# A spline convolution written out as a fixed software pipeline, with the silu products of two strips packed on 64x32 tiles of TensorE

## The chip, the cores and the metric

The kernel is one launch on one core of a Trainium2 chip. The metric is the device time of the launch in microseconds (us); lower is better.

## The reference, cut to what matters

The network has four layers on an array of 8 images, 16 channels and 256 by 256 pixels, each of the form `x = x + layer(groupnorm(x))`: a capsule convolution (layer 0), a spline convolution (layer 1), a patch attention (layer 2) and a 3x3 convolution written with Fourier transforms (layer 3). Only layer 1 is touched:

```
patches = _extract_patches(x, KSIZE, STRIDE, PAD)          # 3x3 neighbourhoods
bspl = _b_splines(patches, grid)                           # 8 cubic splines per value
base_w = base_weight.sum(axis=2)
spl_w = (spline_weight * spline_scaler[..., None]).sum(axis=2)
out = jnp.einsum('bjhwn,ijn->bihw', jax.nn.silu(patches), base_w)
out = out + jnp.einsum('bjhwns,ijns->bihw', bspl, spl_w)
out = out + bias_weight[None, :, None, None]
```

So each output pixel is a 3x3 convolution over 16 channels of silu(x), plus a 3x3 convolution over 16 channels times 8 splines, plus a bias and the residual.

## The kernel before

Layer 1 walks over 8 images of 16 strips each, 128 strips in all; a strip is 16 rows of an image. All data are fp32.

**Per strip, the features.** A tile `xr` holds the input rows of the strip, once for each of four pairs of splines on its 128 partitions. It is worked on in groups of 4 rows pairs, 128x1024 elements each: two groups a strip, and a third, small one (128x256) in the last strip of an image. ScalarE (ACT in the profile) takes two absolute values, `distance` (L1021) and `other` (L1024), into `d`. VectorE (DVE) clips `d` in two ways into `a` and `e` (L1032). ACT squares each into PSUM (`sq`, L1038), DVE multiplies them to cubes (L1041). GpSimd (POOL) subtracts, which gives one half of the splines, `v` (L1050), and DVE makes the other half from it, `m` (`right`, L1053). Both halves lie in a ring of three tiles, `bases`. At the first and last strip of an image a padding row is set as well (`outside`, L1058). ACT also makes two tiles of silu values a strip (L1091).

**Per strip, the products.** One PSUM tile `ps` (one bank; there are two) collects the strip's outputs: 128 partitions are four groups of 32, n = 0 to 3, of two output rows and 16 channels. Each TensorE (PE) product takes a stationary matrix of 128 rows by 32 columns, so four products, n = 0 to 3, lie beside each other on the array. A round is four such products of 512 columns. There are 12 rounds on `bases` (2 values of q, 2 kinds, 3 of dx), the later six of which need the first rows of the next strip too, and three rounds on silu (dx), with a stationary matrix `wm` of 128 rows that holds zeros for the input rows which an output row does not touch. All have the line L1115. Then DVE adds bias and residual (L1152), takes statistics (L1164), and SyncE's queue (SPq) stores the strip.

**Order.** Nothing is written out by hand: each step is handed to a planner, `_Order`, with an estimated duration, its reads and writes and a count of buffers (`places`, `banks`), and the planner sets the order of the instructions on each engine. Its operations with `mode="shared"` are those of DVE and POOL that it keeps apart. The strips are admitted at a period that is given:

```
places = dict(xr=3, d=3, a=3, e=3, res=4, rs=4, y=2)
banks = dict(sq=3, ps=2)
order = _Order({**places, **banks}, 13.3)
```

```
for n in range(len(todo) + 1):
    ...
    if n < len(todo):
        features(*todo[n], op)
    if n:
        conv_strip(*todo[n - 1], op)
    if n < len(todo):
        silus(*todo[n], op)
    ahead(n, op)
```

Ahead of the first strip the weights are summed on PE (L947 and, for silu, L972) and spread by DVE. Within the last strips some steps of layer 2 are run: its norm's statistics (`stats2_steps`), its weights and its first patches. Layer 2 starts once the last strip of layer 1 is stored.

Of the kernel before, what the change touches and what calls it, by code (L numbers as in the profile page):

```python
# [17 lines left out]
P = 128  # L18
# [13 lines left out]
def _consts():  # L32
# [19 lines left out]
    for i in range(C):  # L52
# [32 lines left out]
        "keep": np.stack([p >= 16, p < 112, p >= 64, p < 64], 1),  # L85
# [44 lines left out]
def _layout(w0, bw, sw, sc, bias, wq, bq, wk, bk, wv, bv, w3):  # L130
# [17 lines left out]
    main = np.zeros((8, C, 9, 3, 4, 2, C), np.float32)  # L148
    for ro in range(8):
        for dh in range(3):  # L150

            ri = ro + dh - 1 + (1 if ro < 6 else -1)
            main[ri, :, :, :, ro // 2, ro % 2] = bt[:, :, dh]
    main = main.reshape(P, 9 * 3 * P)
# [151 lines left out]
class _Net:  # L306
# [544 lines left out]
    def layer1(self, bc, bc4, images=range(B), strips=range(16)):  # L851
# [7 lines left out]
        with ExitStack() as st:  # L859
# [3 lines left out]
            wm = one.tile([P, 3, 4, 2 * C], F32, name="wm")  # L863
# [38 lines left out]
            places = dict(xr=3, d=3, a=3, e=3, res=4, rs=4, y=2)  # L902
            banks = dict(sq=3, ps=2)
            order = _Order({**places, **banks}, 13.3)

            def buf(kind, shape):
                n = {**places, **banks}[kind]
                pool = psum if kind in banks else sbuf
                return _Buf(kind, lambda: pool.tile(shape, F32, name=f"{kind}1", tag=kind, bufs=n))

            held = {}

            def edges(i, op):
                def pads():
                    for kind in range(2):
                        for col in (0, WP - 1):
                            nc.gpsimd.tensor_copy(
                                ring[i][:, kind, :, col : col + 1],
                                pad[:, kind : kind + 1].unsqueeze(1).to_broadcast([P, 9, 1]),
                            )  # L920

                op("POOL", 1.0, pads, [], [("place", i)])

            def prepare(op):

                at1, at2 = (ring[i].rearrange("p k m w -> p (k m w)") for i in (1, 2))
                sw, sc, main = at2[:, :2592], at2[:, 2592:3888], at1[:, :3456]
                ws = one.tile([P, 2, 3, 3, C], F32, name="ws")
                wf = ws.rearrange("p k h w o -> p (k h w o)")
                ps = buf("sq", [P, 1024])  # L930
                edges(0, op)

                first = dict(sw=3.5, sc=1.8, main=4.6, b1=0.5)
                for name, t in (("sw", sw), ("sc", sc), ("main", main), ("b1", b1)):
                    op("SP", first[name], lambda name=name, t=t: nc.sync.dma_start(out=t, in_=self.d[name]), [], [(name,)], lag=3.0)

                def scaled():
                    for k in range(2):
                        nc.vector.tensor_tensor(
                            sw[:, k * 1296 : k * 1296 + 1296], sw[:, k * 1296 : k * 1296 + 1296], sc, ALU.mult  # L940
                        )

                def sums():

                    for k in range(2):
                        for m in range(9):
                            nc.tensor.matmul(  # L947
                                ps()[:, k * 144 : k * 144 + 144],
                                self.k["ident"],
                                sw[:, k * 1296 + m * 144 : k * 1296 + m * 144 + 144],  # L950
                                start=m == 0,
                                stop=m == 8,
                            )

                def finish():
                    nc.vector.tensor_copy(wf, ps()[:, :288])
                    nc.vector.tensor_tensor(wf[:, 144:], wf[:, 144:], wf[:, :144], ALU.subtract)
                    nc.vector.tensor_scalar(wf, wf, 1.0 / 6.0, None, ALU.mult)
                    nc.vector.memset(tw, 0.0)

                    for k in range(2):
                        for q in range(2):
                            for h in range(2):
                                for ro in range(2):
                                    dh = 2 * q + h - ro
                                    if 0 <= dh < 3:
                                        lanes = slice(64 * h, 64 * h + 64)
                                        nc.vector.tensor_copy(tw[lanes, k, q, :, ro, :], ws[lanes, k, dh])

                def sums_main():  # L970
                    for m in range(9):
                        nc.tensor.matmul(  # L972
                            ps()[:, 512:896],
                            self.k["ident"],
                            main[:, m * 384 : m * 384 + 384],
                            start=m == 0,
                            stop=m == 8,
                        )

                op("DVE", 2.9, scaled, [("sw",), ("sc",)], [("sw",)], mode="shared")  # L980
                op("PE", 6.0, sums, [("sw",)], [(ps, 0), ("place", 2)])
                op("DVE", 3.5, finish, [(ps, 0)], [("tw",)], mode="shared")
                op("PE", 7.0, sums_main, [("main",)], [(ps, 1), ("place", 1)])


                def finish_main():
                    nc.vector.tensor_copy(wm.rearrange("p d n m -> p (d n m)"), ps()[:, 512:896])

                op("DVE", 0.5, finish_main, [(ps, 1)], [("wm",)], mode="shared")
                for i in (1, 2):  # L990
                    edges(i, op)

            def features(b, j, op):

                i = b * 16 + j
                t = ring[i % 3]
                pairs = 9 if j == 15 else 8
                xr = buf("xr", [P, 9 * W])

                def fetch():  # L1000
                    nc.sync.dma_start(
                        out=xr()[:, : pairs * W],
                        in_=self.x1p[b, :, :, 8 * j : 8 * j + pairs]
                        .rearrange("h c m w -> (h c) (m w)")
                        .unsqueeze(1)
                        .to_broadcast([2 * C, 4, pairs * W]),
                    )

                op("SP", 0.5 if i > 2 else 2.8, fetch, [], [(xr, 0)], lag=6.0 if i else 8.0)
                if not i:  # L1010
                    prepare(op)
                for p in range(0, pairs, 4):
                    n = min(4, pairs - p)
                    us = 0.2 + 0.8 * n / 4
                    d, a, e = buf("d", [P, 1024]), buf("a", [P, 1024]), buf("e", [P, 1024])
                    part = lambda t, n=n: t()[:, : n * W]
                    xn = lambda p=p, n=n: xr()[:, p * W : (p + n) * W]
                    rows = lambda ap: ap.rearrange("p (m w) -> p m w", w=W)

                    def distance(d=d, xn=xn, part=part):  # L1020
                        nc.scalar.activation(part(d), xn(), AF.Abs, bias=bd[:, b : b + 1], scale=sd[:, b : b + 1])  # L1021

                    def other(d=d, part=part):
                        nc.scalar.activation(part(d), part(d), AF.Abs, bias=minus2)  # L1024

                    op("ACT", 1.2 * us, distance, [(xr, 0)], [(d, 0)])
                    op("ACT", 1.15 * us, other, [(d, 0)], [(d, 0)])

                    for q, end, scale in ((a, 2.0, 1.0), (e, 1.0, 2.0)):

                        def less(q=q, d=d, end=end, part=part):
                            nc.vector.tensor_scalar(part(q), part(d), end, end, ALU.min, ALU.subtract)  # L1032

                        op("DVE", 0.68 * us, less, [(d, 0)], [(q, 0)], mode="shared")
                        sq = buf("sq", [P, 1024])

                        def square(q=q, sq=sq, scale=scale, part=part):
                            nc.scalar.activation(part(sq), part(q), AF.Square, scale=scale)  # L1038

                        def cube(q=q, sq=sq, part=part):  # L1040
                            nc.vector.tensor_tensor(part(q), part(q), part(sq), ALU.mult)  # L1041

                        op("ACT", 1.03 * us, square, [(q, 0)], [(sq, 0)])
                        op("DVE", 1.24 * us, cube, [(q, 0), (sq, 0)], [(q, 0)])
# [24 lines left out]
                    if end is not None:  # L1069
                        op("DVE", 0.7, outside, [], [("v", i % 3, p), ("m", i % 3, p)], mode="shared")  # L1070
# [638 lines left out]
```

## Time and profile before

| what | value |
|---|---|
| median of 3 runs | 7611.7 us (7608.63 to 7614.55) |
| the profiled execution | 7613.15 us, of which 7611.4 us are the span that the profiler recorded |
| first to last product of layer 1 (L1115) | from 4343.6 us to 6110.3 us of the span |
| busy in 4343 to 6111 us (1768 us) | PE 1680.3, DVE 1478.1, ACT 1264.9, POOL 737.3 us |
| granted TensorE clock there | 0.98 of full |
| DMA there | 154 GB/s, 0.49 of the engines' time |

How to read it: a row of the groups gives the line, engine and operation, the tiles written and read, the shape (for PE the rows and columns of the stationary matrix, then the moving data), and how often it ran; then busy time and mean time of one instruction. One fp32 product is two matmul records. A record's duration includes a tail in which the next instruction of the engine already runs, so times from start to start are shorter. "Idle before" names what ended a wait. Line numbers are those of the kernel before.

### The profile page before, as it was taken

The page shows a single profiled execution, that of the slowest core. Times are in us where ns is not written, and L with a number is a line of the kernel's source. Part 1 is how long each engine was busy: PE and PEld are TensorE (multiplying, and loading weights), DVE is VectorE, ACT ScalarE, POOL GpSimd, SP SyncE. Part 2 cuts the span into 40 slices and gives each one's busy share as a digit, 9 for nine tenths or more (in the row PEclk, how much of TensorE's full clock was granted, in tenths as well). Part 3 has the DMA queues.
Part 4 walks back from the last instruction along what each step waited for, and adds up shares of the span by engine and source line. Part 5 has one row for each costly group of instructions (what it writes and reads, how often), then busy time and mean ns, then how long its engine had stood idle before and what let it go on. Part 6 is the DMA issues. An engine that isn't in the chain of part 4 may idle for free.

```text
span 7611.4 us, 105952 instructions
## 1 busy us (share of the span) xinstructions
PE 6891.6 (91%) x43144; PEld 3281.4 (43%) x43144; DVE 5416.4 (71%) x6463; ACT 2692.1 (35%) x3834; POOL 3248.3 (43%) x1884
## 2 busy tenths in 40 slices
PE   4888888999989999899998599999999999999999
PEld 1333333333333333333333355444544566666634
DVE  5778888887888888888878788888888833333322
ACT  1222222222222222222222377777777712112200
POOL 0545555555555555555555444444444411111100
PEclk9989999999999999999999699999999999999999
DMA  6222222222222222222222354444445533333277
GB/s 243 66 66 78 78 78 77 77 77 74 77 76 77 76 77 78 78 78 78 78 78 55 103 165 154 151 153 155 150 154 159 159 116 96 86 86 97 67 215 190
DMA packets 451065, 813.01 MB, mean 107 GB/s; under 512 B 57490, under 2 KB 299282, under 8 KB 415250
## 3 DMA queue, kind: packets, MB, share of 16 engines
q1 hardware_dynamic: 380946, 738.85, 33.8%
q10 hardware_dynamic: 69632, 67.39, 3.1%
q8 instruction: 340, 5.57, 0.3%
q14 instruction: 147, 1.20, 0.0%
HBM read 595.63 MB, written 211.03 MB: 106 GB/s over the span
## 4 chain that ended last, share of the span: by engine, by line
PE 52%; POOL 21%; DVE 16%; issue 4%; ACT 3%; DMA 3%; SPq 0%; POOLq 0%; DVEq 0%; ACTq 0%
PE ps L1115 13%; POOL dd L765 11%; PE cv L545 8%; POOL s L765 8%; PE pqk L1474 6%; PE p3s L1585 4%; DVE dd L756 4%; PE cv L549 4%; PE pl L654 3%; PE po L1501 3%; PE pv L1481 3%; PE psc L1489 3%; PE fb L622 3%; POOL s L810 2%; ACT sq L1038 1%
## 5 line engine op out<-in xcount | busy, mean ns | idle before, releaser
L765 POOL TENSOR_TENSOR dd<-dd 128x1024 f32<-128x1024 f32 x512 | 1206.4, 2356 | 1594.9 <-DVE dd L756 1574.8
L1115 PE MATMUL ps<-bases,tw 128*32 128x512 f32 (+1 forms) x13824 | 1379.7, 550 | 89.0 <-DVE bases L1058 71.1
L756 DVE SCALAR_TENSOR_TENSOR dd<-rb,v 128x1024 f32<-128x1024 f32 (+1 forms) x1024 | 1076.9, 1085 | 204.6 <-PE rb L745 194.8
L554 ACT COPY v<-cv 128x1024 f32<-128x1024 f32 x512 | 518.3, 1012 | 1911.0 <-PE cv L549 1911.0
L1050 POOL TENSOR_TENSOR bases<-e,a 128x1024 f32<-128x1024 f32 (+1 forms) x264 | 745.4, 2825 | 1040.5 <-DVE e L1041 870.5
L545 PE MATMUL cv<-kt,w 128*128 128x512 f32 x2048 | 1092.4, 659 | 38.5 <-DVE dd L756 28.7
L1115 PEld LDWEIGHTS ps<-bases,tw 128*32 128x32 f32 x13824 | 734.9, 109 | 743.9 <-issue 442.1
L644 DVE TENSOR_TENSOR pr<-v,fb 128x2048 f32<-128x2048 f32 (+1 forms) x512 | 1020.5, 2017 | 24.9 <-PE pl L654 20.0
L745 PE MATMUL rb<-rs,ct_fold 32*128 32x512 f32 x3584 | 795.8, 657 | 8.3 <-ACT rs L727 2.7
L765 POOL TENSOR_TENSOR s<-s,dd 128x512 f32<-128x512 f32 x512 | 652.0, 1274 | 29.9
L545 PEld LDWEIGHTS cv<-kt,w 128*128 128x128 f32 x2048 | 366.9, 199 | 600.1 <-issue 388.2
L549 PE MATMUL cv<-kt,w 64*128 64x512 f32 x2048 | 590.2, 653 | 0.0
L654 PE MATMUL pl<-pr,ct_fold 128*32 128x512 f32 x3584 | 528.1, 613 | 59.5 <-DVE pr L644 58.7
L1468 POOL TENSOR_TENSOR t<-t,emb 128x512 f32<-128x512 f32 x128 | 161.8, 1264 | 958.4 <-DVE t L1464 943.6
L622 PEld LDWEIGHTS fb<-f,ct_fold 128*128 128x128 f32 x3072 | 377.0, 195 | 340.7 <-issue 299.2
L622 PE MATMUL fb<-f,ct_fold 128*128 128x128 f32 x3072 | 436.5, 290 | 90.1 <-DVE f L608 88.2
L1474 PE MATMUL pqk<-w_qk,t 128*128 128x512 f32 x1024 | 483.0, 594 | 4.4 <-POOL t L1468 4.4
L765 POOL TENSOR_TENSOR s<-v,dd 128x512 f32<-128x512 f32 x256 | 328.7, 1284 | 318.6 <-DVE dd L756 318.5
L1485 ACT ACTIVATE vt<-pv,w_b2v 128x128 f32<-128x128 f32 x512 | 146.0, 368 | 837.0 <-PE pv L1481 837.0
L1505 DVE TENSOR_TENSOR y<-po,res 128x512 f32<-128x512 f32 x128 | 88.5, 692 | 486.8 <-PE po L1501 486.8
L745 PEld LDWEIGHTS rb<-rs,ct_fold 32*128 32x128 f32 x3584 | 240.7, 187 | 380.1 <-DVE dd L756 211.7
L1041 DVE TENSOR_TENSOR e<-e,sq 128x1024 f32<-128x1024 f32 (+1 forms) x264 | 315.2, 1194 | 98.4 <-ACT sq L1038 98.4
(254 smaller groups left out, 9002.0 us busy)
## 6 DMA issues: line engine op xcount, KB each, us to landing
kt<-d SPq DMA_DIRECT2D x256, 516.0 KB
xr<-x1p SPq DMA_DIRECT2D x120, 1024.0 KB
rs<-x SPq DMA_DIRECT2D x256, 256.0 KB
d<-dn ACTq DMA_DIRECT2D x64, 516.0 KB
xs<-in_x_dram SPq DMA_DIRECT2D x16, 2048.0 KB
xs<-in_x_dram SPq DMA_DIRECT2D x64, 512.0 KB
res<-in_x_dram SPq DMA_DIRECT2D x64, 512.0 KB
x<-s SPq DMA_DIRECT2D x128, 256.0 KB
```

The costliest lines, as they stand in the source:

```text
L545: nc.tensor.matmul(ps()[:, n], w[:, 0, j, :], t[:, a : a + 2, 0:W], start=True, stop=False)
L549: nc.tensor.matmul(ps()[:, n], w[at, 1, j, :], t[at, a : a + 2, 2 - n : 2 - n + W], start=False, stop=True)
L554: nc.scalar.copy(v[h]()[:, 4 * g : 4 * g + 4, j * W : j * W + W], ps().rearrange("p n (a w) -> p (n a) w", w=W),)
L622: nc.tensor.matmul(fb()[:, k * P : k * P + P], unfold[:, h, k, :], f()[:, 3], start=True, stop=True)
L644: nc.vector.tensor_tensor(pr()[:, :n], v[h]()[:, 4 * g : 4 * g + n], p().unsqueeze(1).to_broadcast([P, n, 512]), ALU.mult,)
L654: nc.tensor.matmul(pl()[at : at + 32], sel[:, g, h, :], pr()[:, t, :], start=h == 0 and g == 0, stop=h == 1 and (g == 1 or t == 3),)
L745: nc.tensor.matmul(r()[:, n], spread[at, g, h, :], rs()[at], start=True, stop=True)
L756: nc.vector.scalar_tensor_tensor(dd()[:, :n], r()[:, :n], 1.0 / B, v[h]()[:, a : a + n], ALU.subtract, ALU.mult)
L765: op("POOL", us, lambda: nc.gpsimd.tensor_tensor(out[0](), a[0](), b[0](), ALU.add), a[1] + b[1], out[1])
L1050: nc.gpsimd.tensor_tensor(v, rows(part(e)), rows(part(a)), ALU.subtract)
L1115: nc.tensor.matmul(out if k is None else out[:, k], lhs, rhs, start=start, stop=stop, skip_group_check=True)
L1474: nc.tensor.matmul(ps, t[:, n, k * P : (k + 1) * P], wqk[:, n, :], start=n == 0, stop=n == 1)
```

## The change

Layer 1 alone is rewritten; the arithmetic on each value is the same.

- The planner is gone from layer 1. A loop of turns issues the steps in one fixed order. In turn n DVE gets the cubes of strip n, the eviction of strip n-2, `right` of strip n and the clips of strip n+1; ACT one square of strip n, the absolute values of strip n+1, silu of strip n and three squares of strip n+1; POOL the two subtractions of strip n; PE the 12 rounds of strip n-1 and, in odd turns, the silu products of strips n-1 and n.
- The silu products of an even and the odd strip after it are issued together. Each has a stationary matrix of 64 rows by 32 columns. The even strip's silu rows lie in their old order on the partitions; the odd strip's are loaded with the two halves of 64 partitions swapped, so that for each n the two strips use different halves of the array's rows. The zeros in the stationary matrix that filled it to 128 rows are gone. For the odd strip the two loads of silu input become four of half the size.
- The accumulation of an odd strip starts with its silu products and ends with its splines; that of an even strip as before.
- The weights for silu are summed over 96 columns instead of 384, and one of two multiplications of the weights moves from DVE to POOL.
- Buffer counts are as before; the input rows are asked for three strips ahead, right after `right` of the strip that frees the buffer.

```diff
-    main = np.zeros((8, C, 9, 3, 4, 2, C), np.float32)
-    for ro in range(8):
+    main = np.zeros((4, C, 9, 3, 2, C), np.float32)
+    for ro in range(2):
         for dh in range(3):
-            ri = ro + dh - 1 + (1 if ro < 6 else -1)
-            main[ri, :, :, :, ro // 2, ro % 2] = bt[:, :, dh]
-    main = main.reshape(P, 9 * 3 * P)
+            main[ro + dh, :, :, :, ro] = bt[:, :, dh]
+    main = np.tile(main.reshape(64, 9 * 96), (2, 1))
...
-            wm = one.tile([P, 3, 4, 2 * C], F32, name="wm")
+            wm = one.tile([P, 3, 2 * C], F32, name="wm")
...
-            order = _Order({**places, **banks}, 13.3)
...
+            def fetch_raw(n):
+                b, j = todo[n]
+                raws[n] = [make("rs", [P, 2, W]) for _ in range(2)]
+                for r, to in zip((0, 2), raws[n]):
+                    for at, row, k in ((0, r + 4, 4), (64, r, 4)) if n % 2 else ((0, r, 8),):
+                        nc.sync.dma_start(
+                            out=to[at : at + 16 * k].rearrange("p k w -> p (k w)"),
+                            in_=self.x1[j, b, :, row : row + k].rearrange("c r k w -> r c (k w)"),
+                        )
...
+            def squares(n):
+                to_square[n] = [(part, q, scale) for part in parts[n] for q, scale in zip(part[2:4], (1.0, 2.0))]
+                for _ in range(bufs["sq"]):
+                    square(n)
+
+            def cubes(n):
+                for (p, m), part in zip(groups(n), parts[n]):
+                    a, e = part[2:4]
+                    for k, q in enumerate((a, e)):
+                        nc.vector.tensor_tensor(q, q, part[4 + k], ALU.mult)
+                        square(n)
+                    nc.gpsimd.tensor_tensor(ring[n % 3][:, 0, p : p + m, 1 : 1 + W], rows(e), rows(a), ALU.subtract)
...
-                    def last(dx=dx):
-                        for n in range(4):
-                            src = sring[i % 2 * 2 + n // 3]
-                            mm(n, None, wm[:, dx, n], src[:, :, dx : dx + W], stop=dx == 2)
...
+            def silu_products(i):
+                for dx in range(3):
+                    for n in range(4):
+                        for k in (i, i + 1):
+                            half = n // 2 ^ k % 2
+                            at = slice(64 * half, 64 * half + 64)
+                            src = sring[k % 2 * 2 + n % 2]
+                            mm(
+                                k, n, None, wm[at, dx], src[at, :, dx : dx + W], bool(k % 2 and not dx), dx == 2 and not k % 2
+                            )
...
-            with tc.manual_schedule():
-                order.run(sets)
...
+                for n in range(N + 3):
+                    if n < N:
+                        cubes(n)
...
+                    if n + 1 < N:
+                        distances(n + 1)
+                    if 2 <= n < N + 2:
+                        evict(n - 2)
+                    if n < N:
+                        right(n)
+                        for k in range(2 if n == 0 else n + 3, min(n + 4, N)):
+                            fetch_rows(k)
+                        silu(n)
+                        if n + 2 < N:
+                            fetch_raw(n + 2)
+                        if n + 1 < N:
+                            fetch_res(n + 1)
+                    steps = self.ahead1(n, N, images, bases_ps)
+                    if 1 <= n <= N:
+                        for kind, q in ((0, 0), (1, 0), (0, 1), (1, 1)):
...
+                            products(n - 1, kind, q)
...
+                        if n % 2:
+                            silu_products(n - 1)
+                    if n + 1 < N:
+                        clip(n + 1)
+                        squares(n + 1)
```

`ahead1` holds the steps for layer 2 that `ahead` held, at turns 115 to 122 of 128 and at turn 6. `distances`, `clip`, `right`, `silu`, `evict` and `products` hold the instructions of the old L1021/L1024, L1032, L1053/L1058, L1091/L1101, L1152/L1164/L1167 and the first part of L1115.

## The prediction

> **What bounds the kernel now.** I read the page first: layer 1 is the stretch in which L1115 runs, and there PE is the busiest engine. Then the windows of that stretch, which give busy time per engine (PE, PE's weight loads, DVE, ACT, POOL) and, third from the end, the granted clock:
>
> ```profile
> 4343.00:6111.00 1768.00, 1680.27 (x16902) 889.18 (x16902) 1478.07 (x1758) 1264.93 (x1296) 737.31 (x261) 0.98 0.49 154
> 5002.50:5012.70 10.20, 5.00 (x24) 1.35 (x28) 10.16 (x13) 4.57 (x5) 2.48 (x1) 0.50 0.62 201
> 5012.70:5224.30 211.60, 204.87 (x2092) 107.69 (x2084) 176.44 (x209) 155.43 (x161) 90.44 (x33) 1.00 0.47 151
> ```
>
> PE is busy 95% of the stretch. The second row is the start of an image: 10 us at half clock; the third, the rest of that image, runs at full clock. The timeline of PE tells what a strip costs when nothing stalls:
>
> ```profile
> 4946.20 10.54 PE L1115 MATMUL ps<-bases,tw 128*32 128x512 f32 x108
> ...
> 4956.51 2.80 PE L1115 MATMUL ps<-silu,wm 128*32 128x512 f32 x24
> ...
> 4959.08 1.47 PE L1115 MATMUL ps<-bases,tw 128*32 128x512 f32 x11
> ```
>
> From start to start, 12 rounds on bases take 10.31 us and three on silu 2.57: 0.859 a round, 12.88 a strip. The waits of PE say what is added:
>
> ```profile
> PE ps L1115 <- DVE bases L1058: 71.1, 8, 12.9
> PE ps L1115 <- DVE bases L1053: 16.6, 16, 1.8
> ```
>
> The wait for L1058, the padding row, is the one at the ends of images: 12.9 before the first product, the other 58.2 us between images. So 128 x 12.88 = 1649, 58 and 17 of waits, about 10 for layer 2's statistics, and 0.02 of 1768 = 35 for the lowered clock give 1769; the stretch has 1768. The account closes, and PE with its stalls at image ends is the bound.
>
> **What the Trainium skill says.** TensorEngine Tiling (Array Packing), Key Properties: tiles work independently, and changing the tiling mode drains the array. Layer 0 shows both, for other shapes:
>
> ```profile
> 2001.16 1.13 PE L549 MATMUL cv<-kt,w 64*128 64x512 f32 x4
> 2002.22 1.14 PE L745 MATMUL rb<-rs,ct_fold 32*128 32x512 f32 x8
> 2003.29 1.16 PE L622 MATMUL fb<-f,ct_fold 128*128 128x128 f32 x8
> ```
>
> Four records of 64 rows (two products, two passes each) take 1.06 us from start to start, eight records of 32 rows 1.07. Two passes are 0.86; so two and four row tiles ran at once, and a change of mode cost 0.20 us. TensorE: Matmul & The Clock Gate, Part 3, Measured speedup vs the span model, reports 10.6 times for 16 tiles of rows and columns together; no run here shows rows and columns split together, nor in fp32. The same page, What's actually happening, has the clock halved after an idle window; the 0.50 above, behind a stall of some 10 us, agrees. SBUF — State Buffer, section SBUF: two separate sides, says that a POOL operation and a DVE one with two SBUF inputs or in a two-port mode exclude each other for a whole instruction. The trace agrees (POOL and DVE timelines):
>
> ```profile
> 4979.98 2.38 POOL L1050 TENSOR_TENSOR bases<-e,a 128x1024 f32<-128x1024 f32 x1 [5.54 <-PE ps L1115]
> ...
> 4980.06 2.45 DVE L1032 TENSOR_SCALAR e<-d 128x256 f32<-128x256 f32 x1
> ```
>
> That clip is a 128x256 one, whose neighbours take 0.29 us: it waited for POOL.
>
> **The change, part by part.**
>
> *Silu on PE.* 24 products a pair, as before, but eight tiles at a time instead of four: three rounds a pair, 2.57 us, for six, 5.15. Two mode changes a pair at 0.20 take back 0.40. PE then has 10.31 and 10.31 + 2.97 = 13.28 us in even and odd turns, 11.80 a strip, 188.7 an image. Bounds: at worst tiles run one after another (rival C), at best the mode changes are free (11.60).
>
> *DVE's turn.* Steps from start to start, in this timeline of DVE:
>
> ```profile
> 4989.06 0.69 DVE L1032 TENSOR_SCALAR a<-d 128x1024 f32<-128x1024 f32 x1
> 4989.67 0.70 DVE L1032 TENSOR_SCALAR e<-d 128x1024 f32<-128x1024 f32 x1
> 4990.27 1.23 DVE L1041 TENSOR_TENSOR a<-a,sq 128x1024 f32<-128x1024 f32 x1
> 4991.40 1.22 DVE L1041 TENSOR_TENSOR e<-e,sq 128x1024 f32<-128x1024 f32 x1
> ```
>
> A clip 0.60, a cube 1.13, and by the same reading `right` 1.19, the eviction 0.80 and its statistics 0.60. A turn is 4 cubes 4.52, eviction 1.40, two `right` 2.38, four clips 2.40: 10.70. To this comes the lock. POOL's second subtraction starts some 0.26 after the fourth cube, at 4.78, and holds the port 2.17, to 6.95; `right` would start at 5.92 and waits 1.03. So 11.73 a turn. Nothing moves past that: the clips come after `right`, cubes and eviction don't use the port. At an image's end the third group and the padding rows add: POOL 0.55, `right` 0.39, rows 0.64 twice, clips 0.40, silu rows 0.52, aggregation 0.5, together 3.6 (its cubes, 0.66, lie under POOL's work). An image is 16 x 11.73 + 3.6 = 191.3 us on DVE.
>
> *The order.* PE's 188.7 and DVE's 191.3 are within 1.4%; what joins them decides whether the larger one is reached. The eviction of turn n waits for PE's turn n-1, and behind it stand `right`, the clips and the next cubes; as `right` waits for POOL anyway, PE may end up to 5.5 us into DVE's turn for nothing. PE in its turn needs POOL's first subtraction (done at 4.9 us of DVE's turn) after 5.2, and the first `right` (8.1) after 7.7: it must run at least 0.4 behind. Between 0.4 and 5.5 there is room for the 3 us by which PE's turns differ. The stalls at image ends (58) and the half clock behind them (35) should shrink to waits of 1 to 2 us, since the third group now costs DVE 3.6 and the lag is a reserve. I add 0.7 an image for what slips: 192.
>
> *ACT* has four squares at 0.95, absolute values 2 x (1.26 + 1.06), silu 2 x 0.71: 9.9 of 12 us. Its last square waits for a PSUM bank that the first cube frees, 1.2 us into the turn, and is needed at 3.4: covered. *POOL* has two subtractions, 4.8 us. *SP's queue* has 5 issues in even and 7 in odd turns (the split silu loads count) at 0.6: 3.0 to 4.2 us. The next input rows stand behind `right` and are needed after 17 us; their first load took 5.6 us in the prologue. DMA's share of 0.49 rises to about 0.56. All three I put at nothing under DVE's cover; if a load were late, ACT's absolute values would be, with 3 us of slack.
>
> *Before the first strip.* 18 matmuls of 384 columns (5.82 us) become 96 columns, about 3.7, and DVE's spreading no longer waits for them (it did for 5.2). DVE's turn 1 starts at about 4335 instead of the first product's 4343.6.
>
> *Sum.* Turn 128 would start at 4335 + 8 x 192 - 12 = 5859; PE is 2 us behind and has 10.3 left, the last eviction 0.9: 5872. Before, the last eviction ended at 6111.2, and layer 2 starts off it in both. 239 us less than the profiled execution's 7613.15 (its span and 1.75 around it; 1.5 over the median of 7611.7): **7374 us**.
>
> **Rivals.** *A: DVE's loop is longer than its steps.* Every turn has some eight waits on other engines, and both loops are nearly full, so slips add up. For it: before, DVE's busy time per strip was 11.6, not 10.7. Against it: that holds the locks. At 0.6 more a turn, 128 x 0.6 = 77: 7451. *B: the change doesn't do what it says:* only four tiles run at once. Then silu costs 5.15 + 0.40 a pair, PE 13.08 a strip, 209.3 an image: 7374 + 8 x 17.3 = 7512; only the stalls at image ends are won. *C, slower: fewer than four.* The two strips of a pair write the same 32 partitions, in two banks. If fp32 products on 64x32 tiles run two at a time, the most that the trace shows for 64 rows, 24 products cost 12 rounds, 10.3 us a pair, PE 15.66 a strip, 250.6 an image: 7374 + 8 x 58.6 = 7843. It decides from an image of 192 + 239/8 = 221.9, where silu costs 6.7 us a pair: below 3.1 tiles at a time the kernel is slower. Against B and C: column tiles of four and row tiles of two and four both ran at full rate.
>
> **How the numbers follow.** The forecast has 0.70, A 0.13, B 0.08, C 0.06; 0.03 is for what I don't see. A change under 0.2%, about what a measurement of this kernel can tell from none, would need a half-way case between B and C: 0.02. Faster 0.91, slower 0.07. The range starts where PE's 188.7 with nothing lost is the bound (8 x 3.3 = 26 less, 7348) and takes in A: 7345 to 7460, leaving out B and C.
>
> **What would show it.** Right: 64*32 silu records, 24 products in about 3.0 us with the mode changes; no wait of PE over 3 us between images and the clock at 1.00; `right` waiting about 1 us for POOL; layer 1 over at about 5872. Wrong in A: DVE with idle time ahead of evictions or cubes. Wrong in B or C: silu stretches of 5.5 or 10 us. Wrong in the order: PE waiting each turn for `right` or POOL.

## The result, and the profile after

The changed kernel takes 7392.2 us (median of 4 runs, 7387.6 to 7396.3), the kernel before beside it 7613.1: a ratio of 0.971, 95% interval 0.9693 to 0.9727. The prediction was 7374, range 7345 to 7460: the right side and mechanism, 18 us too low. The profiled execution took 7396.3 us, with a span of 7394.5; against the span of before that is 216.9 us less. Layer 1's last eviction ends at 5893.9 us instead of 6111.2, 217.3 earlier, so the whole gain lies in layer 1.

The windows of layer 1 in the changed kernel (columns as before: length, busy time of PE, weight loads, DVE, ACT and POOL, clock, DMA share, GB/s): the whole layer, then the stretches in which one image ends and the next begins. PE works a strip behind DVE and comes to the new image a turn after it, in the last two rows.

```profile
4344.00:5894.00 1550.00, 1535.07 (x16874) 646.45 (x16866) 1529.14 (x1753) 1274.57 (x1300) 616.84 (x262) 1.00 0.54 175
5095.00:5106.00 11.00, 11.00 (x125) 3.81 (x121) 10.96 (x15) 8.81 (x10) 3.65 (x3) 1.00 0.49 152
5106.00:5117.00 11.00, 11.00 (x120) 4.83 (x116) 10.93 (x15) 8.07 (x9) 3.70 (x2) 1.00 0.45 151
5117.00:5310.00 193.00, 191.43 (x2112) 80.93 (x2108) 192.35 (x221) 160.71 (x164) 77.71 (x33) 1.00 0.53 175
```

PE and DVE are both busy 99% of the layer, and the clock stays at full speed through the change of image. PE's waits there are short:

```profile
5120.30 2.78 PE L1020 MATMUL ps<-bases,tw 128*32 128x256 f32 x30 [0.90 <-POOL bases L989]
5123.73 1.50 PE L1020 MATMUL ps<-bases,tw 128*32 128x256 f32 x15 [0.65 <-DVE bases L997]
```

Busy time can't say which of the two is the bound here; the waits and the steps of the loop have to. The timeline of PE over a pair of strips:

```profile
4355.24 20.97 PE L1020 MATMUL ps<-bases,tw 128*32 128x512 f32 x216
4376.14 2.81 PE L1020 MATMUL ps<-silu,wm 64*32 64x512 f32 x48
4378.88 1.50 PE L1020 MATMUL ps<-bases,tw 128*32 128x512 f32 x12
```

The silu products of two strips, 48 records, take 2.74 us from start to start, and a pair 4378.88 - 4355.24 = 23.64, or 11.82 a strip. The timelines of DVE and POOL over one turn (the counterpart of the DVE steps shown of before):

```profile
4933.90 1.21 DVE L987 TENSOR_TENSOR a<-a,sq 128x1024 f32<-128x1024 f32 x1
4935.03 1.21 DVE L987 TENSOR_TENSOR e<-e,sq 128x1024 f32<-128x1024 f32 x1
...
4938.42 0.86 DVE L1059 SCALAR_TENSOR_TENSOR y<-ps,b,res 128x256 f32<-128x256 f32 x2
4939.32 0.70 DVE L1067 BATCH_NORM_STATS2 st<-y 128x6 f32<-128x512 f32 x1
4939.93 3.49 DVE L997 SCALAR_TENSOR_TENSOR bases<-xr,xm,bases 128x1024 f32<-128x1024 f32 x2
4943.35 0.68 DVE L966 TENSOR_SCALAR a<-d 128x1024 f32<-128x1024 f32 x1
...
4945.76 1.21 DVE L987 TENSOR_TENSOR a<-a,sq 128x1024 f32<-128x1024 f32 x1
```

```profile
4936.41 4.74 POOL L989 TENSOR_TENSOR bases<-e,a 128x1024 f32<-128x1024 f32 x2 [7.12 <-DVE e L987]
```

A turn is 4945.76 - 4933.90 = 11.86 us. DVE never stands idle in it by the record, yet the two `right` (L997) take 3.42 from the first's start to the clip, where two free ones take 2.38: the first waits inside its record until POOL's second subtraction, whose record ends at 4941.15, gives up the port. It is the port that it waits for and not a result: the first `right` reads what POOL's first subtraction wrote, and only the second `right` reads the second. At the start of an image, where a padding row lies between the two `right`, the trace has them apart; the first is stretched, the second is not:

```profile
5108.46 2.32 DVE L997 SCALAR_TENSOR_TENSOR bases<-xr,xm,bases 128x1024 f32<-128x1024 f32 x1
...
5111.47 1.28 DVE L997 SCALAR_TENSOR_TENSOR bases<-xr,xm,bases 128x1024 f32<-128x1024 f32 x1
```

So a turn is a ring through two engines: DVE's first two cubes until POOL starts (2.51 us), POOL's subtractions until the port is free (4943.35 less the 2.38 of the two `right` is 4940.97, so 4.56), the two `right` (2.38) and the clips (2.41), 11.86 in all. The other two cubes and the eviction run beside POOL's work (the fourth cube is ready for POOL at about 4.78 us, 0.26 after its end, just ahead of the 4.86 at which POOL takes it). Turn 1, which has no eviction, takes 11.78 all the same (4341.92 to 4353.70). The waits of layer 1:

```profile
PEld ps L1020 <- DVE bases L997: 40.7, 63, 1.1
...
DVE y L1059 <- PE ps L1020: 11.8, 2, 8.9
...
PE ps L1020 <- POOL bases L989: 6.9, 9, 0.9
PE ps L1020 <- DVE bases L997: 5.8, 9, 0.7
```

PE's weight loads wait for `right` once in each of 63 pairs, 0.65 us on average, and DVE waits for PE twice in the whole layer, 8.9 of the 11.8 us ahead of the very last eviction. So DVE's loop, with POOL's subtractions in it, is the bound, by a hair. The padding row's wait, 71.1 us before, is gone from the list; what is left of it is 4.0 us ahead of the first product. The page's chain of the work that ended last, over all four layers and by engine, moves the same way (before: PE 52%, DVE 16%):

```profile
PE 40%; DVE 28%; POOL 21%; issue 6%; DMA 3%; ACT 1%; SPq 0%; DVEq 0%; POOLq 0%; ACTq 0%
```

### The profile page after: what moved, and what is told of

It is laid out like the page before. It is cut to its first block, busy times and chain, and to the rows that moved or that the text cites. A ratio compares the mean times of both kernels' runs of the same rounds, so it can differ in the third digit from the quotient of the medians.

```text
span 7394.5 us, 105976 instructions
## 1 busy us (share of the span) xinstructions
PE 6744.3 (91%) x43144; PEld 3035.6 (41%) x43144; DVE 5467.2 (74%) x6462; ACT 2697.9 (36%) x3834; POOL 3127.8 (42%) x1885
## 3 DMA queue, kind: packets, MB, share of 16 engines
q14 instruction: 148, 1.21, 0.1%
## 4 chain that ended last, share of the span: by engine, by line
PE 40%; DVE 28%; POOL 21%; issue 6%; DMA 3%; ACT 1%; SPq 0%; DVEq 0%; POOLq 0%; ACTq 0%
POOL dd L764 11%; POOL s L764 8%; PE cv L544 8%; PE pqk L1441 6%; DVE bases L997 6%; DVE dd L755 4%; PE p3s L1552 4%; PE cv L548 4%; DVE e L987 4%; PE pl L653 3%; PE po L1468 3%; PE pv L1448 3%; PE psc L1456 3%; PE fb L621 3%; DVE a L987 2%
## 5 line engine op out<-in xcount | busy, mean ns | idle before, releaser
L1020 PE MATMUL ps<-bases,tw 128*32 128x512 f32 (+1 forms) x13824 | 1361.9, 546 | 16.8 <-POOL bases L989 6.9
L755 DVE SCALAR_TENSOR_TENSOR dd<-rb,v 128x1024 f32<-128x1024 f32 (+1 forms) x1024 | 1075.5, 1083 | 205.8 <-PE rb L744 193.9
L989 POOL TENSOR_TENSOR bases<-e,a 128x1024 f32<-128x1024 f32 (+1 forms) x264 | 621.5, 2377 | 929.4 <-DVE e L987 929.1
L1020 PEld LDWEIGHTS ps<-bases,tw 128*32 128x32 f32 x13824 | 595.4, 109 | 804.7 <-issue 485.1
L997 DVE SCALAR_TENSOR_TENSOR bases<-xr,xm,bases 128x1024 f32<-128x1024 f32 (+1 forms) x264 | 447.8, 1735 | 0.3 <-POOL bases L989 0.3
```

Of the source, the lines that this page charges most:

```text
L755: nc.vector.scalar_tensor_tensor(dd()[:, :n], r()[:, :n], 1.0 / B, v[h]()[:, a : a + n], ALU.subtract, ALU.mult)
L989: nc.gpsimd.tensor_tensor(ring[n % 3][:, 0, p : p + m, 1 : 1 + W], rows(e), rows(a), ALU.subtract)
L997: nc.vector.scalar_tensor_tensor(r, rows(part[1]), xm[:, b : b + 1], v, ALU.is_gt, ALU.mult)
L1020: nc.tensor.matmul(out if k is None else out[:, k], lhs, rhs, start=start, stop=stop, skip_group_check=True)
```

## The experiments

The kernel before ran at 7615.1 to 7615.8 us (medians) beside the groups of these; times are medians. "An image" is 16 turns, from first cube to first cube.

**Order without the packing.** All of the change, but with the stationary matrix of silu again 128 rows high, so that four tiles run at once.

```diff
-                            at = slice(64 * half, 64 * half + 64)
+                            at = slice(0, 128)
```

> The fixed order without the packing: each silu product takes all 128 rows again, so six rounds a pair of strips instead of three and no change of tiling mode (the sums take in rows of the other half as well, so the silu part of the result is another one). Theory (two gains: the packing shortens PE's path, the order takes away the stalls at image ends): PE is the bound again with 12.88 us a strip, 206.1 an image against 193.3, so 8 x 12.8 = 102 us over the changed kernel, about 7495 (7480 to 7510), still some 118 faster than before; no wait of PE over 3 us between images, clock at 1.00. Rival 1 (DVE alone bounds the changed kernel by a wide margin, the packing is idle): within 20 us of 7392. Rival 2 (the order brings nothing, all comes from the packing): 7570 to 7611.

Measured: 7496.5 us, ratio 0.9845 (0.983 to 0.9859). The windows:

```profile
4344.00:5880.00 1536.00, 1535.37 (x15686) 781.01 (x15682) 1376.55 (x1641) 1205.08 (x1224) 577.21 (x245) 1.00 0.52 166
```

PE is busy 1535.4 of 1536 us at full clock and DVE has slack: with the order alone, PE is the bound and is held up for 0.6 us in all. The order, with the shorter preparation of the silu weights, is worth 7615.7 - 7496.5 = 119 us, and the packing, on top of it, 104. The 119 lie near the 58 + 17 + 35 = 110 us that the account of the kernel before put down to PE's waits and the lowered clock.

**The planner with less work on PE.** The kernel before, with half of the silu rounds left out (so 1.3 us a strip less on PE, about what packing gives), at the old period and at a shorter one. By its code the period doesn't admit strips (at most four are open at a time): it sets how far apart the due times of successive strips lie, and among the steps that could start the planner takes the one due first.

```diff
-                for dx in range(3):
+                for dx in (0, 2) if i % 2 else (2,):
...
-            order = _Order({**places, **banks}, 13.3)
+            order = _Order({**places, **banks}, 12.0)    # second kernel only
```

> The planner's kernel of before with PE relieved by what the packing saves: the silu rounds are 1 and 2 in turn instead of 3 (half of the silu products are left out), 11.60 us of PE a strip; the planner's period stays 13.3. Theory (the planner's order keeps its stalls at image ends, 58 us and 35 of lowered clock, and runs into the lock of DVE and POOL): 128 x 1.29 = 165 us less at best, 7448, and rather 7450 to 7520. Rival 1 (the order is worth nothing once PE is relieved): 7392 or less. Rival 2 (the planner can't use the relief at all): 7580 to 7611.

> As the run before with the planner's period at 12.0 instead of 13.3 (half of the silu products are left out here too), so that its ranks fit the shorter strip. Theory: as there, 7450 to 7520, within 30 us of it either way, since the period only ranks what is ready. Rival: the period is what holds the planner back, and the time comes to 7392 or less.

Measured: 7794.5 us at 13.3 (ratio 1.0233, 1.0218 to 1.0248) and 7851.0 at 12.0 (1.0306, 1.0289 to 1.0323). Both are slower than the kernel before, with less to do; neither a theory nor a rival had that. The windows and waits at 13.3:

```profile
4343.00:6290.00 1947.00, 1645.45 (x15350) 624.37 (x15342) 1430.11 (x1752) 1272.11 (x1295) 606.97 (x262) 0.96 0.51 139
```

```profile
PEld ps L1115 <- POOL bases L1050: 321.6, 170, 3.6
...
DVE bases L1053 <- POOL bases L1050: 204.0, 83, 2.9
PE ps L1115 <- POOL bases L1050: 175.7, 118, 2.7
```

No engine is full any more. PE waits for the first half of the splines, as does DVE in `right`; POOL's subtractions come late, and a strip takes 14.9 us (one POOL subtraction starts at 4999.87, its counterparts of the next two strips at 5014.85 and 5029.66). So relief of this size on PE does not pay under the planner as it stood: the order that it makes for the changed costs is a worse one. The packing itself was not run under the planner, and which of its choices makes the order worse was not tried.

**Which loop is the bound.** Three kernels that leave out work, on top of the change. First, one of three silu rounds (dx = 1), which relieves PE alone:

```diff
-                for dx in range(3):
+                for dx in (0, 2):
```

> The changed kernel with two silu rounds a pair instead of three (the middle column of the silu filter is left out): PE 11.4 us a strip instead of 11.82, DVE untouched at 11.87. Theory (DVE's turn is the bound, by a hair): 7380 to 7395. Rival (PE is the bound): 64 x 0.86 = 55 us less, 7337.

Second, from strip 3 on, the lower half of POOL's second subtraction of each strip, which relieves DVE of the wait for the port and PE of nothing; third, both.

```diff
-                    nc.gpsimd.tensor_tensor(ring[n % 3][:, 0, p : p + m, 1 : 1 + W], rows(e), rows(a), ALU.subtract)
+                    h = 2 if p == 4 and n > 2 else m
+                    nc.gpsimd.tensor_tensor(
+                        ring[n % 3][:, 0, p : p + h, 1 : 1 + W], rows(e)[:, :h], rows(a)[:, :h], ALU.subtract
+                    )
```

> The changed kernel with POOL's second subtraction of each strip half as long from the fourth strip on (the other half of those spline values is left as an earlier strip wrote it). Everything that DVE and PE run is as it was; only the port is free 1.1 us earlier. Theory (DVE waits about 1.1 us a turn for the port and that wait is on the path): DVE's turn falls to about 10.8 us, PE becomes the bound with 11.82 a strip, 189.1 an image against 193.3, so 8 x 4.2 = 34 us less: 7358 (7350 to 7368). Rival 1 (the wait lies beside something else of the same length): 7385 to 7395. Rival 2 (PE is not next, the loops let DVE run free): 7392 - 128 x 1.07 = 7255.

> Both of them: POOL's second subtraction half as long, and two silu rounds a pair instead of three (the same parts left out as in those two runs). Theory (the two loops stand within 0.5% of each other, so only relief of both pays fully): PE 11.4 a strip, 182.2 an image, DVE about 176: 8 x 11 = 89 us less than the changed kernel, 7303 (7290 to 7320), more than the sum of the two single runs' gains. Rival (independent gains): the sum of the two single runs' gains.

Measured: less on PE 7392.9 (ratio 0.9708), that is nothing; a shorter subtraction 7354.0 (0.9656, 0.9643 to 0.9669), 38 us less than the changed kernel; both 7303.1 (0.9589, 0.9576 to 0.9602), 89 less. Two edits that give 0 and 38 alone and 89 together are the mark of two loops that lie close: taking from the longer one helps until the other holds. DVE's timeline with the short subtraction:

```profile
4954.24 2.47 DVE L1000 SCALAR_TENSOR_TENSOR bases<-xr,xm,bases 128x1024 f32<-128x1024 f32 x2
```

The two `right` take 2.47 instead of 3.49: the 1.0 us that they had lost was the lock, and an image fell to 188.4 us, which is PE's.

**The same, with nothing left out.** If POOL's second subtraction of a strip is put off to the start of the next turn, it lies under DVE's cubes, which don't need the port (a cube takes 1.21 us in the changed kernel, beside a subtraction or not). Its `right` follows it, the input rows are asked for behind that, the eviction goes behind `right`, and PE takes its products in an order that needs the late half last. (A one-element copy keeps POOL from starting early, under the clips.)

```diff
+            def later(n):
+                return 0 <= n < len(todo) and todo[n][1] < 14
...
+                    if later(n - 1):
+                        nc.gpsimd.tensor_copy(token, parts[n][-1][3][:, :1])
+                        subtract(n - 1, (True,))
                     if n < N:
                         cubes(n)
+                        subtract(n, now)
...
+                    if later(n - 1):
+                        right(n - 1, (True,))
+                    if n < N:
+                        right(n, now)
...
                     if 2 <= n < N + 2:
                         evict(n - 2)
...
-                        for kind, q in ((0, 0), (1, 0), (0, 1), (1, 1)):
+                        for kind, q in ((0, 0), (0, 1), (1, 0), (1, 1)):
```

> A full version without the wait: POOL's second subtraction of a strip is put off to the next turn's start (a one-element copy on POOL that reads the last clip keeps it from starting earlier), where DVE's cubes don't use the port; the right half of these rows follows on DVE in that turn ahead of the eviction, and PE takes the products in the order that this allows. The two last strips of an image keep the old order. Theory (the lock wait was on the path and PE is next): DVE's turn 11.2 us, PE the bound with 11.82, 7358 to 7370. Rival 1 (the later right half makes PE wait, PE's room in DVE's turn being used up): 7392 or more. Rival 2 (the input rows, freed later by half a turn, arrive late): ACT waits for DMA some us a turn, 7420 or more.

Measured: 7392.1 us (0.9705, 0.9692 to 0.9718), no gain, where 7358 to 7370 was expected. The trace shows a gain that is mostly given back: DVE's turn fell from 11.87 to 11.24 and an image from 193.4 to 190.4 us, but the two turns at each image's end, whose strips are not put off, rose to 15.0 and 15.3 us, and the last image took 199.1 us for the 15 turns that took 185.4 in the changed kernel. Three kernels followed: no putting off in the last image; on top of that, putting off all strips of the other seven, with small clip buffers of their own for an image's third group; and on top of that, the weights' second multiplication back on DVE.

```diff
-                return 0 <= n < len(todo) and todo[n][1] < 14
+                return 0 <= n < len(todo) - 16                 # first kernel: also todo[n][1] < 14
...
-                        q = make(kind, [P, 1024])[:, : d.shape[1]]
+                        few = d.shape[1] == W
+                        q = make(kind + "3", [P, W]) if few else make(kind, [P, 1024])[:, : d.shape[1]]
...
-                    (nc.vector, nc.gpsimd)[k].tensor_tensor(part, part, sc, ALU.mult)
+                    nc.vector.tensor_tensor(part, part, sc, ALU.mult)        # third kernel only
```

> The put-off POOL subtraction of e6 for the strips 0 to 13 of the first seven images only; the last image in the order of the changed kernel. In e6 an image of PE and DVE together took 190.4 us instead of 193.3, but the last image 199.1 instead of some 185: PE stands still in it behind late input rows (ACT waits 23 us for xr), which are asked for a turn later when their strip's right is put off, at a time when the next layer's loads share the DMA. If that is the whole loss: 7 x (193.3 - 190.4) = 20 us off 7392, that is 7372. Rival: the last image loses by the new order of products (the statistics steps of layer 2 in between), which stays in this kernel: then still some 14 us lost there, 7386.

> As e7a, but all 16 strips of the first seven images are put off; the third, small group of an image's last strip gets clip buffers of its own (256 columns), so that three large ones are enough. This takes away the two turns of 15 us at the image ends of e6. Theory (after that PE alone is the bound): a pair of turns 23.56, an image 188.5 to 188.8, 7 x (193.3 - 188.8) = 31 us off 7392, and one turn longer by 3 before the last image: 7364. Rival (image ends still cost DVE their 3.4 us, and PE waits for it): as e7a, 7372.

> e7b with both multiplications of the weights on DVE ahead of the first strip, as before the change. Theory: POOL's multiplication held a clip of DVE for 2.7 us in the prologue; without it DVE pays 1.5 us for the second multiplication, so that the weight sums start 1 to 3 us earlier and the whole is 1 to 3 us shorter than e7b. Rival: the start of the first strip is set by loads, and nothing moves (within 1 us).

Measured: 7400.4, 7386.1 and 7385.2 us. The images behaved (190.4 us in the first, 188.6 in the others, as predicted), the last image did not: 205.8, 210.9 and 208.7 us, worse than with the putting off. Late input rows, my theory, had not been the whole loss, and the rival's 14 us were too few; most of its turns took 13.3 to 13.4 us, those without any step of layer 2 too. (In the version before these three ACT did wait 23.4 us for `xr` in the last image, against 7.9 in the whole layer of the changed kernel. How much of that image's loss this was, no run tells.) The multiplication: from the last statistics product of layer 0 (start 4308.95 and 4312.16 us) to the first product of layer 1 (4341.95 and 4341.72) the trace has 33.0 us with POOL and 29.6 with DVE. But layer 0 ended 3.2 later in that execution, and the medians differ by 0.9: the prologue is shorter in the trace, and the time doesn't resolve it.

The order of products was the rival of the first of these, so I put the old one back for the last image's strips, all else as in the third kernel.

```diff
-                        for kind, q in ((0, 0), (0, 1), (1, 0), (1, 1)):
+                        for kind, q in ((0, 0), (0, 1), (1, 0), (1, 1)) if later(n - 1) else ((0, 0), (1, 0), (0, 1), (1, 1)):
```

> e7c with the products of the last image's strips in the old order ((0,0), (1,0), (0,1), (1,1)), as their subtractions are not put off either; all other strips as in e7c. Theory: in e7a to e7c the turns of the last image took 13.4 us instead of 11.9 because the new order asks for the next strip's POOL subtraction as the second group of products, which an order that doesn't put off anything delivers too late; with the old order the last image takes the 185.4 us that it took in the changed kernel, plus some 2 to 4 for the turn that joins the two orders: 208.7 becomes 189, 20 us off 7385, that is 7365. Rival (the last image is slow through the loads of layer 2 and its statistics steps, whatever the order): over 7380.

Measured: 7382.1 us, the last image 209.4: a miss, it was not the order of products. DVE's timeline in the last image shows the reason:

```profile
5829.48 4.58 DVE L1010 SCALAR_TENSOR_TENSOR bases<-xr,xm,bases 128x1024 f32<-128x1024 f32 x2 [0.31 <-POOL bases L993]
5833.99 0.86 DVE L1075 SCALAR_TENSOR_TENSOR y<-ps,b,res 128x256 f32<-128x256 f32 x2
```

In rewriting the turn I had put the eviction behind `right`. Where the subtraction is not put off, the eviction and its statistics, 1.5 us that don't use the port, then no longer lie under POOL. The port comes free no earlier: the `right` wait longer, 4.58 us instead of 3.49 and behind an idle gap, and the turn grows by the 1.5 us, from 11.87 to 13.37. The last kernel puts the eviction first again in those turns.

```diff
+                    if 2 <= n < N + 2 and not later(n):
+                        evict(n - 2)
                     if later(n - 1):
                         right(n - 1, (True,))
...
-                    if 2 <= n < N + 2:
+                    if 2 <= n < N + 2 and later(n):
                         evict(n - 2)
```

> e8 with the eviction ahead of right again in the turns of the last image, as in the changed kernel. In e8 those turns were still 13.35 us: two rights took 4.58 us from the first's start, 2.1 of them the wait for POOL's port, where they take 3.49 in the changed kernel, because the eviction with its statistics (1.4 us), which does not use the port, lay behind them instead of under POOL's first subtraction. Theory: a turn falls back to 11.9, the last image from 209.4 to some 187 to 189, 21 us off 7382, that is 7361. Rival (what lengthens the last image is something else): over 7376.

Measured: 7361.0 us (7359.1 to 7369.8), ratio 0.9669 (0.9656 to 0.9682), as expected. It is faster than both the kernel before and the changed one: 31 us, 0.42%, under the latter by the medians, and the intervals of the two ratios don't overlap. The last image is down to 188.5. The windows over the first seven images, then the timelines of PE and of DVE and POOL:

```profile
4340.00:5660.00 1320.00, 1319.59 (x14782) 585.62 (x14778) 1280.92 (x1534) 1127.32 (x1145) 551.47 (x342) 1.00 0.55 182
```

```profile
4936.78 2.81 PE L1036 MATMUL ps<-silu,wm 64*32 64x512 f32 x48
4939.52 20.88 PE L1036 MATMUL ps<-bases,tw 128*32 128x512 f32 x216
4960.32 2.81 PE L1036 MATMUL ps<-silu,wm 64*32 64x512 f32 x48
```

```profile
4938.70 2.87 DVE L1010 SCALAR_TENSOR_TENSOR bases<-xr,xm,bases 128x1024 f32<-128x1024 f32 x2
4941.49 0.86 DVE L1075 SCALAR_TENSOR_TENSOR y<-ps,b,res 128x256 f32<-128x256 f32 x2
```

```profile
4934.53 4.76 POOL L993 TENSOR_TENSOR bases<-e,a 128x1024 f32<-128x1024 f32 x2
```

POOL now ends at 4939.29, and `right` loses 0.4 us instead of 1.0. PE is busy 1319.6 of 1320 us, at 4960.32 - 4936.78 = 23.54 a pair; 8 x 23.54 = 188.3, and an image takes 188.6. PE is the bound, with nothing between its products.

## Why the prediction was right, and where it was 18 us short

- **Silu, eight tiles at a time: right.** 2.57 + 0.40 for the mode changes was put down for a pair; the silu stretch took 2.74 from start to start. PE came to 11.82 a strip against 11.80. Rivals B and C would have needed stretches of 5.5 or 10 us. With the packing undone the kernel was at 7496.5, near B's 7512: B described a kernel that exists, but not this one.
- **The lock: right.** `right` loses 1.0 us to POOL's second subtraction, in every turn; the short subtraction took it away and gave 38 us, where 34 were expected. What the Trainium skill says (SBUF — State Buffer, section SBUF: two separate sides), that such operations of the two engines exclude each other for a whole instruction, holds here: the wait is 3.42 - 2.38 = 1.04 us, and it moves with the end of POOL's work, to 4.58 - 2.47 = 2.1 us where the eviction is taken from between. That 1.04 agrees so well with the 1.03 of the sum is luck: the port came free about 0.1 us later than put down, and the eviction with its statistics, 1.51 us instead of 1.40, brought `right` to it 0.1 later.
- **The turn: mis-sized by 0.11 us on average.** 11.73 was the sum of DVE's steps and the lock, and 12.0 with image ends and slip; DVE took 11.86 in a plain turn, and 12.11 on average from turn 1 (4341.92) to turn 127 (5868.15). The step that failed is the start of POOL's second subtraction. I put it 0.26 after the fourth cube, at 4.78 us of the turn, to hold the port to 6.95. POOL is still in its first one then (my own 4.9 for the end of that one said so): the two run one behind the other, the second starts at 4.86, and the port comes free at 7.07, some 0.2 before POOL's record ends at 7.25. That is 0.12 in every plain turn; with the clips' 2.41 it makes 11.86. Image ends give back a little of it, and the slip set aside was needed too, for turns with steps of layer 2. From turn 1 to turn 127 it comes to 126 x 0.11 = 14 us. The eviction's extra 0.1 costs nothing, as it lies under the wait.
- **Image ends: right.** 3.6 us extra were expected and 3.3 measured (turns of 12.27, 13.76 and 12.91 in place of three of 11.87). PE's waits of 58 us and the half clock of 35 became a wait of 0.90 and one of 0.65 at the image start shown, at clock 1.00.
- **Before the first strip: mis-sized by 7 us.** Turn 1 started at 4341.9, not 4335. Layer 0 ended 2.7 later in this execution (its last statistics product started at 4310.46, before at 4307.81). Most of the rest is, by the traces, the multiplication that moved from DVE to POOL, which I had not costed: it held the port, and a clip of 0.69 took 3.41. With it back on DVE that clip took 0.69 again, and turn 1 came 26.9 to 27.2 us after layer 0's last statistics product in three kernels, instead of 30.2 to 30.3 in the three others that put off. (The medians of the two that differ in this alone are only 0.9 apart, so the whole time doesn't confirm it.) About 1 us stays unexplained. The 96-column matmuls took 2.14 us, not 3.7, but no one waited for them: DVE was spreading the other weights until 4335.8.
- **The sum.** 7 + 14 + 1 = 22 us: the last eviction at 5893.9 instead of 5872. By the medians it is 18, since the profiled execution was 4 over the median.
- **Covered work: right.** ACT, POOL's sum, SP's queue and DMA (share 0.54 for about 0.56) set nothing; ACT's waits for `xr` in the whole layer were 7.9 us. Rival A, a DVE loop with slips of 0.6 a turn, did not come: DVE waits for PE 11.8 us in all.

Both misses of the sum, apart from the 2.7 us by which layer 0 ended later, are uses of the shared port by POOL: in the turn I had the port free 0.12 us too early, and ahead of the first strip I had not followed the moved multiplication at all.

## What to carry to other kernels

Where two engines are nearly even, busy time names no bound: take from each loop alone and from both, and the three times tell how far apart they are. Look also at where a loop runs: here it went through two engines, and the steps beside its way, such as the eviction, cost nothing until they were moved onto it. An order planned for one set of costs need not suit another: the planner's became 2.3% slower when PE had less to do, and 3.1% with its period at 12.0. A lock between two engines is a matter of place: put the instructions that don't need the shared port under the one that holds it, and recheck what lies there each time an instruction moves. When a partial change gives nothing, measure the loop piece by piece (plain turns, ends, the last image) before dropping it: here a gain of 3 us an image was mostly paid back in the last image, and in the kernels that followed an eviction that had moved cost some 20 us there.

## What the runs showed of the hardware

- Eight fp32 tiles of 64 by 32 ran side by side at the full rate: 48 records, three rounds, took 2.74 us, where three rounds of 0.859 are 2.58. In the last kernel, where PE has no gaps, a pair takes 23.54 us and 27 rounds of 0.859 are 23.19: 0.35 us at most for both changes of mode, near the two times 0.20 read from layer 0.
- One POOL multiplication of 128x1296 took a clip of DVE from 0.69 to 3.41 us, though the two touch different tiles.
- By the record DVE went on some 0.2 us before POOL's subtraction ended (port free at 7.07 us of the turn, record's end at 7.25), and the time that DVE waited for the port counts as busy in its own record: two `right` of 2.47 us show as 3.49.
